# First loads over two queues, a copy moved behind the first products, and another order of the last group's products

## The chip, the cores and the metric

The kernel runs on one core of a Trainium2 chip. The core has a matrix engine (TensorE, PE in the tables), a vector engine (VectorE, DVE), a scalar engine (ScalarE, ACT), a general one (GpSimd, POOL) and SyncE (SP), which only issues transfers. Each engine works through its own list of instructions in order, and the engines wait for one another by semaphores. ACT, SP and POOL can issue DMA transfers: an issue stands in the engine's list like any other instruction. On chip lie SBUF (128 partitions) and PSUM, the small memory into which PE writes and accumulates.

The metric is device time in microseconds (us), the median over several executions; less is better.

## The reference

Two graph layers over N = 4096 nodes with 512 features and one 0/1 adjacency matrix, each followed by a residual and a layer norm. Cut to what matters here, the first layer is:

```
support = (x @ weight).reshape(N, 4, 128)          # 4 heads
f1 = <support, weight_u> per head;  f2 = <support, weight_v> per head
w = leaky_relu(f1[j] + f2[i], 0.2) * adj[i, j]
attn = softmax over j of w, where w != 0
out = attn @ support + bias + x @ proj_w + proj_b
x1 = layernorm(x + out)
```

The second layer is masked attention with 8 heads of 64 over x1, with keys, queries and values from Wks, Wqs, Wvs and an output projection Wo. The change touches the first layer alone, at its very beginning and at the end of its first stage.

## The kernel before

The order of the work on every engine is the order of the program's text (a manual schedule); only semaphores are put in by the framework.

The first stage, the group stage, computes support and the base rows (x + x @ proj_w + biases) for 8 groups of 512 rows (`NG` groups of `GT` = 4 tiles). The two products x @ weight (kind "s") and x @ proj_w (kind "b", where `add_identity`, L888, adds the identity to proj_w so that x itself is included) are each done with a scheme of seven block products instead of eight. So a group has 14 products, named s1 to s7 and b1 to b7, each 8 matmul records on PE (L844). They need sums and differences of weight blocks (`combine_w`, L761, on DVE for "s" and on POOL for "b") and of blocks of x (`combine_x`, L795 to L802). x comes as blocks into `y_sb` (`load_x`, L652) and is turned by 32 x 32 transposes on DVE into `xT` (`turn_x`, L738).

`product` (L844 to L878) runs one product and what follows it. Products 1, 5, 6 and 7 open a PSUM tile (of six, `o_ps`); 2 goes on in the tile of 1, 3 in that of 5, 4 in that of 7. Before 2, 3 or 4 may accumulate, the tile's earlier value must have been read: 1 and 5 are copied out by ACT (L861), 7 is read by a DVE add (L867), and 6 by another (L865). Product 2 is copied by ACT into its place (L863), 3 and 4 are finished by a DVE add (L872). For "b", 3 and 4 end with POOL adding the bias (L876) and SP storing the base rows (L878).

`dots` (L815) is a set of eight dot products on DVE of one quarter of the group's support with u and v, which gives f1 and f2. u and v are spread over all partitions, loaded into `uv` in SBUF and copied once by ACT into PSUM (`uv_ps`, tile x_ps, L901), from where DVE reads them.

The order of the 14 products of a group is a list, `begin` for the first group and `usual` for the others. `todo` puts each quarter's dots a fixed number of places behind the product that completes it. At places 0, 3, 7 and 10 of each list work of later stages is slipped in (`beside`). In the last group place 7 holds two conversions of adjacency (L601, ACT) and `front` of the first three attention steps: ACT computes signs `z` (L628), DVE masks `az` (L632) and the weights `p` (L637).

`factors` follows a group: ACT takes exponentials of f, POOL scales the support (L694 to L698), SP stores it (L701), and DVE turns the factor rows (L708), which SP stores (L713). For all groups but the last it is put off into the next group; for the last it stands right behind the 14 products.

Then come the attention passes: for each step PE multiplies `p` with the scaled support (L1062). In the first pass SP still issues adjacency transposes (L595) for the last pieces of the first window, in its order behind the stores of the last group's `factors`, and ACT converts them (L601) ahead of the steps that use them.

The very first instructions are transfers. SP sends x of group 0 in eight pieces (two halves of four), then the right halves of weight and proj_w in 16 pieces, u, v, and x of group 1. ACT sends the left halves in 16 pieces and the bias. `load_w0` (L661) sends one piece: 64 rows of one half of the columns, 64 KB, into 32 partitions. Then, in the text, DVE turns x of group 0, POOL and DVE combine weights, ACT copies u and v (L901), and the products begin.

Of the kernel before, what the change touches and what calls it, by code (L numbers as in the profile page):

```python
# [12 lines left out]
AF = mybir.ActivationFunctionType  # L13
# [416 lines left out]
def tile_gat_then_masked_attention(  # L430
# [16 lines left out]
    nc = tc.nc  # L447
    N, D = x.shape
    H0, D0, _ = weight_u.shape
# [3 lines left out]
    NG = N // G  # L453
# [15 lines left out]
    SQ = 32  # L469
    NQ = P // SQ  # L470
    HG = G // 2
    HD = D // 2
# [32 lines left out]
    def on_all_partitions(src, n):  # L505
        return bass.AP(tensor=src.tensor, offset=src.offset, ap=[[0, P], [1, n]])
# [63 lines left out]
    with tc.tile_pool(name="l0", bufs=NG) as l0, \  # L570
# [71 lines left out]
        with tc.tile_pool(name="l0s", bufs=2) as sp:  # L642
            w_sb, pw_sb = (sp.tile([P, KC, D], F32, name=n, bufs=1) for n in ("w_sb", "pw_sb"))
            uv = sp.tile([P, 2, D], F32, name="uv", bufs=1)
            ys, xTs = {}, {}

            def load_x(g, b0=0, b1=G // SQ):

                if g not in ys:
                    ys[g] = sp.tile([P, G // SQ, P], F32, name="y_sb", bufs=3)  # L650
                for a in range(NQ):
                    nc.sync.dma_start(  # L652
                        ys[g][a * SQ:(a + 1) * SQ, b0:b1, :],
                        x[g * G + b0 * SQ:g * G + b1 * SQ, a * P:(a + 1) * P].rearrange(
                            "(b r) f -> r b f", r=SQ))

            def load_w0(queue, dst, src, c, m):

                for a in range(NQ):
                    f = a * P + 2 * c * SQ  # L660
                    queue.dma_start(  # L661
                        dst[a * SQ:(a + 1) * SQ, 2 * c:2 * c + 2, m * HD:(m + 1) * HD],
                        src[f:f + 2 * SQ, m * HD:(m + 1) * HD].rearrange("(k r) d -> r k d", r=SQ))

            bb = sp.tile([P, D], F32, name="bb", bufs=1)
            for n in range(2):
                load_x(0, n * HG // SQ, (n + 1) * HG // SQ)
            for queue, m, srcs in ((nc.scalar, 0, ((w_sb, weight), (pw_sb, proj_w))),
                                   (nc.sync, 1, ((w_sb, weight),)),
                                   (nc.sync, 1, ((pw_sb, proj_w),))):  # L670
                for c in range(2):
                    for dst, src in srcs:
                        load_w0(queue, dst, src, c, m)
            nc.scalar.dma_start(bb, on_all_partitions(bias, D))
            nc.sync.dma_start(uv[:, 0, :], on_all_partitions(weight_u, D))
            nc.sync.dma_start(uv[:, 1, :], on_all_partitions(weight_v, D))
            load_x(1)

            def factors(g, s4):
# [83 lines left out]
            def w_of(kind, i):  # L763
                w = w_sb if kind == "s" else pw_sb
                if i in (1, 2, 3):
                    return w_block(w, *{1: (0, 0), 2: (1, 0), 3: (1, 1)}[i])
                return sums_w[kind][{5: 0, 6: 1, 7: 2, 4: 3}[i]]
# [36 lines left out]
            def x_of(g, i):  # L804
                if i in (1, 2, 4):
                    return x_block(g, *{1: (0, 0), 2: (0, 1), 4: (1, 1)}[i])
                return x_s[g][{5: 0, 6: 1, 7: 2, 3: 3}[i]]
# [25 lines left out]
            def product(g, s4, kind, i):  # L833

                if i in (1, 5, 6, 7):
                    tiles[kind, i] = op.tile([P, G], F32, name="o_ps")
                out = tiles[kind, {2: 1, 3: 5, 4: 7}.get(i, i)]
                more = i in (2, 3, 4)  # L840
                xb, wb = x_of(g, i), w_of(kind, i)
                for t in range(2):
                    for c in range(2):
                        nc.tensor.matmul(out[:, t * HD:(t + 1) * HD], xb[:, c, t * P:(t + 1) * P],  # L844
                                         wb[:, c, :], start=not more and t == 0 and c == 0,
                                         stop=c == 1, skip_group_check=True)
                if i == 1:
                    if kind == "b":
                        for n in range(2):
                            base[n] = sp.tile([P, 2, D], F32, name="base", bufs=2)  # L850
                    elif g == NG - 1:
                        places = room("y_sb").rearrange("p s c r -> p s (c r)")
                        sb.update({("s", 1): places[:, 0], ("s", 5): places[:, 1],
                                   ("b", 1): places[:, 2], ("b", 5): places[:, 3]})
                    else:
                        sb.update({("s", 1): room("z"), ("s", 5): room("z"),
                                   ("b", 1): room("az"), ("b", 5): room("az")})
                u2, p5 = sb[kind, 1], sb[kind, 5]
                last = block_of(kind, s4, 1, 1)
                if i in (1, 5):  # L860
                    nc.scalar.activation(sb[kind, i], out, AF.Copy)  # L861
                elif i == 2:
                    nc.scalar.activation(block_of(kind, s4, 0, 0), as_block(out, kind), AF.Copy)  # L863
                elif i == 6:
                    nc.vector.tensor_tensor(u2, out, u2, op=ALU.add)  # L865
                elif i == 7:
                    nc.vector.tensor_tensor(last, as_block(out, kind), as_block(u2, kind),  # L867
                                            op=ALU.add)
                    nc.gpsimd.tensor_tensor(last, last, as_block(p5, kind), op=ALU.add)
                else:  # L870
                    n, m = (0, 1) if i == 3 else (1, 0)
                    nc.vector.tensor_tensor(block_of(kind, s4, n, m), as_block(out, kind),  # L872
                                            as_block(u2, kind), op=ALU.add)
                if kind == "b" and i in (3, 4):
                    n = (3, 4).index(i)
                    nc.gpsimd.tensor_tensor(base[n], base[n],  # L876
                                            bb[:, None, :].to_broadcast([P, 2, D]), op=ALU.add)
                    nc.sync.dma_start(base_d[g][:, 2 * n:2 * n + 2, :], base[n])  # L878
# [18 lines left out]
            combine_w(nc.gpsimd, "b", (5, 6, 7, 4))  # L897
            nc.gpsimd.dma_start(bb, on_all_partitions(proj_b, D), accum_op=ALU.add)
            uv_ps = [xp.tile([P, H0, D0], F32, name="x_ps") for _ in range(2)]
            for k in range(2):  # L900
                nc.scalar.activation(uv_ps[k], uv[:, k, :].rearrange("p (h d) -> p h d", h=H0),  # L901
                                     AF.Copy)
            usual = [(kind, i) for i in (1, 5, 2, 6, 7, 3, 4) for kind in ("s", "b")]
            begin = [("s", 1), ("b", 1), ("s", 2), ("b", 2), ("s", 5), ("s", 6), ("s", 7),
                     ("b", 5), ("s", 3), ("b", 6), ("s", 4), ("b", 7), ("b", 3), ("b", 4)]
            for g in range(NG):
                fs[g] = l0.tile([P, 2, GT, H0], F32, name="f")
                s4 = sp.tile([P, H0, GT, W0], F32, name="s4")
                plan = usual if g else begin
                todo = {}  # L910
                for i, wait, n, m in ((2, 1, 0, 0), (3, 0, 0, 1), (7, 3, 1, 1), (4, 0, 1, 0)):
                    todo.setdefault(plan.index(("s", i)) + wait, []).append((n, m))
                for k, (kind, i) in enumerate(plan):
                    if k in (0, 3, 7, 10):
                        t = (0, 3, 7, 10).index(k)
                        if t == 1 and g + 2 < NG:
                            load_x(g + 2)
                        for fn in beside.get(g * GT + t, []):
                            fn()
                    product(g, s4, kind, i)  # L920
                    for nm in todo.get(k, ()):
                        dots(g, s4, *nm)
                    first = 0 if g else 10
                    if g + 1 < NG and first <= k < first + KC:
                        turn_x(g + 1, k - first)
                    if g + 1 < NG and (6 <= k < 10 if g else k == 13):
                        for n in (k - 6,) if g else range(4):
                            combine_x(g + 1, n)
                    if k in (2, 6, 9, 13):
                        later.step()  # L930
                xTs.pop(g)
                x_s.pop(g)
                if g + 1 < NG:
                    later.at(1, lambda g=g, s4=s4: factors(g, s4))
                else:
                    factors(g, s4)
# [18 lines left out]
        with wait_by_tile("l0v", 2) as vp:  # L955
# [95 lines left out]
            for n, (w, h, j) in enumerate(steps):  # L1051
# [7 lines left out]
                p = p_t.pop((w, h, j))  # L1059
                s = sup[w * H0 + h, j // GT][:, j % GT, :]  # L1060
# [507 lines left out]
```

## Time and profile before

| what | value |
|---|---|
| median of 3 runs | 3373.38 us (3373.2 to 3379.11) |
| the profiled execution's own time | 3375.75 us |
| its span | 3374.0 us |
| PE busy | 3321.3 us, 98% of the span |
| DVE, POOL, ACT busy | 2362.1, 2227.8, 1987.5 us |
| first product on PE | 7.72 us after the span's start |
| last product of the last group | 221.21 us |
| first attention step on PE | 222.93 us |

The span is the time from the first to the last instruction in the profile; the execution's own time lies 1.75 us above it. PE is the engine that is nearly always busy, and the second layer takes most of the span. Matmul ends are modelled, so a busy PE does not mean that its clock is full: the clock that was granted stands in a column of its own in the tables by stretches of time. A row "PE o_ps <- ACT z" in a table of waits says that a PE instruction on tile o_ps was released by an ACT instruction on tile z. A tile name is that of the program; a place can serve under several names (the tile z holds the copy of s1 in the first groups).

### The profile page before, as it was taken

How to read it: one execution, taken by the hardware profiler on the slowest of the kernel's cores; microseconds unless marked ns; L12 is line 12 of the kernel's file. 1: busy time of each engine (PE TensorE's matmuls, PEld its weight loads, DVE VectorE, ACT ScalarE, POOL GpSimd, SP SyncE). 2: the span in 40 equal slices, each digit the busy share in tenths (PEclk: the TensorE clock that was granted, in tenths of full speed). 3: DMA queues.
4: the chain of work that ended last, by engine and by line, in shares of the span. 5: the costliest groups of instructions: out<-in, count | busy, mean ns of one | idle time of the engine just before them, and what ended most of it. 6: DMA issues, size and time to landing. Idle time of an engine off the chain costs nothing.

```text
span 3374.0 us, 66618 instructions
## 1 busy us (share of the span) xinstructions
PE 3321.3 (98%) x27050; PEld 1946.6 (58%) x27050; DVE 2362.1 (70%) x2892; ACT 1987.5 (59%) x2463; POOL 2227.8 (66%) x1590
## 2 busy tenths in 40 slices
PE   7999999999999999999999999999999999999998
PEld 6889999999999855643333333333333333333332
DVE  5678999898898711156766667676676666667666
ACT  1247877878776421155665656656566656656563
POOL 4550031040030275579999999999999999999996
PEclk9999999999999999999999999999999999999999
DMA  7978869769441443388889888889888889798984
GB/s 149 231 163 185 198 184 216 147 161 215 140 130 64 101 162 112 124 217 197 210 191 220 226 209 194 208 196 241 212 189 212 191 207 252 186 210 189 211 195 109
DMA packets 400334, 620.41 MB, mean 184 GB/s; under 512 B 166928, under 2 KB 249872, under 8 KB 398992
## 3 DMA queue, kind: packets, MB, share of 16 engines
q0 software_dynamic: 97520, 258.77, 42.1%
q1 hardware_dynamic: 300544, 354.92, 34.0%
q8 instruction: 215, 3.52, 0.4%
q10 hardware_dynamic: 1952, 2.36, 0.3%
q14 instruction: 103, 0.84, 0.1%
HBM read 315.87 MB, written 117.64 MB: 128 GB/s over the span
## 4 chain that ended last, share of the span: by engine, by line
PE 92%; DMA 3%; POOL 2%; DVE 2%; issue 1%; ACT 1%; SPq 0%; ACTq 0%; POOLq 0%; DVEq 0%
PE o_ps L1062 26%; PE o_ps L1375 24%; PE s_ps L1113 24%; PE s_ps L1178 5%; PE o_ps L844 5%; PE s_ps L1439 3%; PE s_ps L1171 3%; DMA p<-p 2%; POOL q_sum L1350 1%; PE s_ps L1394 1%; DVE p L637 0%; PE x_ps L1043 0%; POOL p L1360 0%; DMA stage<-adj_d 0%; DMA k_d<-v_sb 0%
## 5 line engine op out<-in xcount | busy, mean ns | idle before, releaser
L1350 POOL TENSOR_TENSOR q_sum<-q_sum,p 128x1024 f32<-128x1024 f32 x538 | 1374.5, 2555 | 67.4 <-DMA p<-p 37.2
L1330 DVE TENSOR_TENSOR p<-s_ps,adjT 128x1024 f32<-128x1024 f32 x896 | 1044.6, 1216 | 468.2 <-ACT s_ps L1327 433.2
L1327 ACT ACTIVATE s_ps<-s_ps 128x1024 f32<-128x1024 f32 x1021 | 967.4, 1006 | 599.1 <-PE s_ps L1113 598.9
L1113 PE MATMUL s_ps<-q_sb,k_sb 64*64 64x512 f32 x8192 | 943.3, 589 | 4.2 <-DVE p L1330 4.2
L1375 PE MATMUL o_ps<-p,v_sb 64*64 64x512 f32 x8192 | 943.6, 590 | 0.0
L1062 PE MATMUL o_ps<-sup_t,p 128*128 128x129 f32 x8192 | 920.5, 275 | 6.2 <-DVE p L637 6.1
L1062 PEld LDWEIGHTS o_ps<-sup_t,p 128*128 128x128 f32 x8192 | 917.3, 192 | 7.3 <-DVE p L637 7.2
L637 DVE SCALAR_TENSOR_TENSOR p<-fr_t,dj,az 128x1024 f32<-128x1024 f32 x512 | 656.0, 1291 | 78.6 <-PE o_ps L1062 51.4
L1113 PEld LDWEIGHTS s_ps<-q_sb,k_sb 64*64 64x64 f32 x8192 | 312.2, 133 | 571.2 <-issue 451.2
L1375 PEld LDWEIGHTS o_ps<-p,v_sb 64*64 64x64 f32 x8192 | 310.1, 133 | 570.7 <-issue 560.8
L628 ACT ACTIVATE z<-fr_t,f 128x1024 fp8e4<-128x1024 f32 x512 | 558.0, 1144 | 117.5 <-DVE az L632 117.2
L1360 POOL DMA_DIRECT2D p<-p x412 | 439.0, 1305 | 10.2 <-PE o_ps L1375 8.6
L1026 POOL DMA_DIRECT2D agg<-base_d x32 | 28.7, 1208 | 516.0 <-ACT agg L1012 515.8
L1330 DVE TENSOR_TENSOR p<-s_ps,md 128x1024 f32<-128x1024 f32 x128 | 151.0, 1218 | 68.8 <-ACT s_ps L1327 62.3
L632 DVE TENSOR_TENSOR az<-adjT,z 128x512 int32<-128x512 int32 x256 | 175.7, 686 | 7.5 <-ACT z L628 6.8
L588 POOL COPY seen<-token 128x1 f32<-128x1 f32 x24 | 14.0, 582 | 245.9 <-DVE token L586 245.9
L1185 ACT ACTIVATE sb<-s_ps 128x1024 f32<-128x1024 f32 x35 | 35.8, 1024 | 192.6 <-PE s_ps L1178 129.8
L601 ACT ACTIVATE adjT<-stage 128x1024 fp8e4<-128x1024 bf16 x128 | 130.5, 1050 | 9.2 <-DMA stage<-adj_d 9.2
L1200 POOL TENSOR_TENSOR sb<-sb,sb 128x1024 f32<-128x1024 f32 x36 | 85.0, 2374 | 72.2 <-ACT sb L1185 72.2
L1224 DVE COPY k_sb<-s_ps 128x1024 f32<-128x1024 f32 x12 | 14.7, 1225 | 141.4 <-PE s_ps L1178 91.8
L1439 PE MATMUL s_ps<-wo_sb,on 128*128 128x512 f32 x240 | 110.8, 604 | 0.0
L1409 ACT ACTIVATE r<-r_h 32x256 f32<-32x256 f32 x248 | 102.3, 412 | 2.9
(176 smaller groups left out, 2133.4 us busy)
## 6 DMA issues: line engine op xcount, KB each, us to landing
p<-p POOLq DMA_DIRECT2D x412, 512.0 KB, 9.1
k_sb<-k_d SPq DMA_DIRECT2D x128, 512.0 KB
v_sb<-v_d SPq DMA_DIRECT2D x128, 512.0 KB
adj_d<-in_adj_dram POOLq DMA_DIRECT2D x32, 1024.0 KB, 10.7
sup_t<-sup_d SPq DMA_DIRECT2D x120, 258.0 KB
fr_t<-fr_d SPq DMA_DIRECT2D x16, 1024.0 KB
adjT_d<-adjT SPq DMA_DIRECT2D x32, 512.0 KB
adjT<-adjT_d SPq DMA_DIRECT2D x32, 512.0 KB
```

The lines of the kernel that those rows point to most:

```text
L628: nc.scalar.activation(z[:, k, :], fr[:, 0, :], AF.Sign, bias=fs[j // GT][:, 0, (j + k) % GT, h:h + 1], saturate=False)
L632: nc.vector.tensor_tensor(az.bitcast(I32), adjT[w, j // CJ][:, j % CJ:j % CJ + 2, :].bitcast(I32), z.bitcast(I32), op=ALU.bitwise_and)
L637: nc.vector.scalar_tensor_tensor(p, fr[:, 1, :], dj[j // GT][:, j % GT, h:h + 1], az_t[w, h, j // 2][:, j % 2, :], op0=ALU.max, op1=ALU.mult)
L844: nc.tensor.matmul(out[:, t * HD:(t + 1) * HD], xb[:, c, t * P:(t + 1) * P], wb[:, c, :], start=not more and t == 0 and c == 0, stop=c == ...
L1062: nc.tensor.matmul(o[t // BK][:, t % BK, :], p[:, t * P:(t + 1) * P], s, start=(j == 0 and t % BK == 0), stop=(j == NT - 1), skip_group_ch ...
L1113: nc.tensor.matmul(s[c:c + MS, e, :], k[r, a + c:a + c + MS], qt[g, m][r, :], start=True, stop=True)
L1327: nc.scalar.activation(s, s, AF.Exp)
L1330: nc.vector.tensor_tensor(p, s, keep[:, None, :].to_broadcast([P, HP, G]), op=ALU.mult)
L1350: nc.gpsimd.tensor_tensor(q, q, p, op=ALU.add)
L1360: later.at(2, lambda: nc.gpsimd.dma_start(a, b, accum_op=ALU.add))
L1375: nc.tensor.matmul(o[c, n, :], v[r, j % CH, c], p[r, e, :], start=(j == 0), stop=(j == NT - 1))
L1439: nc.tensor.matmul(s, on_t[g][:, m, t * P:(t + 1) * P], wo_sb[:, m, :], start=(m == 0), stop=(m == NP1 - 1))
```

## The change

Three things change.

- First loads. `load_w0` sends whole rows, 64 rows of all 512 columns, 128 KB in one piece. All 16 pieces go on ACT's queue: the first half of the rows of weight, then of proj_w, then the second halves. u, v and the bias follow on ACT's queue. On SP's queue x of group 1 now follows x of group 0.
- The copies of u and v into PSUM move from ahead of all products to behind the third product (s2) of the first group, ahead of the first dots.
- The last group gets its own order, `end`.

```
-            def load_w0(queue, dst, src, c, m):
+            def load_w0(dst, src, c):
                 for a in range(NQ):
                     f = a * P + 2 * c * SQ
-                    queue.dma_start(
-                        dst[a * SQ:(a + 1) * SQ, 2 * c:2 * c + 2, m * HD:(m + 1) * HD],
-                        src[f:f + 2 * SQ, m * HD:(m + 1) * HD].rearrange("(k r) d -> r k d", r=SQ))
+                    nc.scalar.dma_start(
+                        dst[a * SQ:(a + 1) * SQ, 2 * c:2 * c + 2, :],
+                        src[f:f + 2 * SQ, :].rearrange("(k r) d -> r k d", r=SQ))
...
-            for queue, m, srcs in ((nc.scalar, 0, ((w_sb, weight), (pw_sb, proj_w))),
-                                   (nc.sync, 1, ((w_sb, weight),)),
-                                   (nc.sync, 1, ((pw_sb, proj_w),))):
-                for c in range(2):
-                    for dst, src in srcs:
-                        load_w0(queue, dst, src, c, m)
+            for c in range(2):
+                for dst, src in ((w_sb, weight), (pw_sb, proj_w)):
+                    load_w0(dst, src, c)
+            for k, src in enumerate((weight_u, weight_v)):
+                nc.scalar.dma_start(uv[:, k, :], on_all_partitions(src, D))
             nc.scalar.dma_start(bb, on_all_partitions(bias, D))
-            nc.sync.dma_start(uv[:, 0, :], on_all_partitions(weight_u, D))
-            nc.sync.dma_start(uv[:, 1, :], on_all_partitions(weight_v, D))
             load_x(1)
...
-            for k in range(2):
-                nc.scalar.activation(uv_ps[k], uv[:, k, :].rearrange("p (h d) -> p h d", h=H0),
-                                     AF.Copy)
...
+            end = [("s", 1), ("b", 1), ("s", 5), ("s", 2), ("s", 6), ("s", 7), ("b", 5),
+                   ("s", 3), ("b", 2), ("s", 4), ("b", 6), ("b", 7), ("b", 3), ("b", 4)]
...
-                plan = usual if g else begin
+                plan = end if g == NG - 1 else usual if g else begin
...
                     product(g, s4, kind, i)
+                    if g == 0 and k == 2:
+                        for n in range(2):
+                            nc.scalar.activation(uv_ps[n], uv[:, n, :].rearrange(
+                                "p (h d) -> p h d", h=H0), AF.Copy)
```

## The prediction

> **What bounds the kernel now.** I read first who keeps TensorE (PE) waiting over the whole kernel. A row gives the waiting engine, tile and line, whom it waited for, microseconds in all, times, and the longest.
>
> ```profile
> PE o_ps L844 <- ACT z L861: 14.7, 1, 14.7
> PE o_ps L844 <- DVE xT L738: 7.7, 1, 7.7
> PE o_ps L1062 <- DVE p L637: 6.1, 4, 2.9
> ...
> PE o_ps L844 <- DVE base L867: 1.7, 1, 1.7
> ```
>
> PE is busy 3321.3 of 3374.0 us, so a change that adds no PE work can win only some 50 us. All four rows lie before 263 us; behind that PE hardly waits, so a shift there reaches the end whole. Next, the start: PE's instructions in order of time, then ScalarE's (ACT), each row start, length, engine, line.
>
> ```profile
> 7.72 3.78 PE L844 MATMUL o_ps<-w_sb,xT 128*128 128x256 f32 x8 [7.72 <-DVE xT L738]
> 11.29 1.98 PE L844 MATMUL o_ps<-pw_sb,xT 128*128 128x256 f32 x8
> 28.00 3.78 PE L844 MATMUL o_ps<-w_sb,xT 128*128 128x256 f32 x8 [14.73 <-ACT z L861]
> 31.57 2.08 PE L844 MATMUL o_ps<-pw_sb,xT 128*128 128x256 f32 x8
> ```
> ```profile
> 10.94 0.44 ACTq L674 DMA_DIRECT2D bb<-in_L_gnn_bias_dram  x1
> 11.41 1.28 ACT L901 ACT_TABLE_LOAD   x1 [11.41 <-DMA pw_sb<-in_L_gnn_proj_w_dram]
> 23.93 0.60 ACT L901 ACTIVATE x_ps<-uv 128x512 f32<-128x512 f32 x1 [11.24 <-DMA uv<-in_L_gnn_weight_u_dram]
> 26.83 0.60 ACT L901 ACTIVATE x_ps<-uv 128x512 f32<-128x512 f32 x1 [2.29 <-DMA uv<-in_L_gnn_weight_v_dram]
> 27.36 0.58 ACT L861 ACTIVATE z<-o_ps 128x512 f32<-128x512 f32 x1
> ```
>
> Product s1 was ready at 11.5, but its copy (27.36) stood on ACT behind the two copies of uv, the last data to land. Product s2 accumulates in the same PSUM tile and waited for that copy. PE's restart costs more: s2 took 3.78 us, where later products take 1.89. Stretches of 2 us (last three columns: granted PE clock, DMA share, GB/s) give the clock and the DMA rate.
>
> ```profile
> 8.00:10.00 2.00, 2.00 (x5) 1.56 (x6) 0.64 (x2) 0.00 (x0) 0.00 (x0) 1.00 1.17 201
> 10.00:12.00 2.00, 2.00 (x7) 1.67 (x6) 0.00 (x0) 0.59 (x1) 0.43 (x2) 1.00 1.10 208
> 18.00:20.00 2.00, 0.00 (x0) 0.00 (x0) 2.00 (x3) 0.00 (x0) 1.81 (x2) 0.57 0.52 135
> 28.00:30.00 2.00, 2.00 (x5) 1.64 (x6) 0.00 (x0) 0.43 (x1) 1.05 (x2) 0.50 1.19 194
> ```
>
> DMA runs at 201 to 208 GB/s while x and weights come together, 135 when SP alone sends 64 KB pieces. The mean clock of 0.57 in 18 to 20 puts its fall near 18.3, 5 us after PE's last work at 13.3. Third, the last group, from the timelines of DVE, GpSimd (POOL), SP and PE.
>
> ```profile
> 227.96 3.35 DVE L637 SCALAR_TENSOR_TENSOR p<-fr_t,dj,az 128x1024 f32<-128x1024 f32 x1
> ```
> ```profile
> 227.87 2.35 POOL L876 TENSOR_TENSOR base<-base,bb 128x1024 f32<-128x1024 f32 x1 [2.30 <-DVE base L872]
> ```
> ```profile
> 241.63 12.46 SPq L595 DMA_TRANSPOSE stage<-adj_d  x2
> ```
> ```profile
> 258.76 41.42 PE L1062 MATMUL o_ps<-sup_t,p 128*128 128x129 f32 x365 [1.09 <-DVE p L637]
> ```
>
> DVE ends the group at 227.96 with p of attention step 3. POOL adds the bias to the base rows, scales the support until 238.4, SP stores it, and only then issues the adjacency transposes. Their landing lets ACT go on at 252.5, and PE's last wait here ends at 258.76.
>
> **The change, part by part: first loads.** SP loses 16 weight DMAs and u, v; ACT keeps 16 weight DMAs, of 128 instead of 64 KB, and gains u and v: 16 + 2 + bias = 19 issues, all ahead of its first arithmetic. At 0.44 us each they would take 8.4 us, but issues wait for landings: SP's queue waited 2.3 us for w_sb before x pieces (L652). The first eight issues of both queues together go without such waits, and the ninth on wait, which I read as a count of eight open DMAs shared by both queues. The order along that count seems to follow bytes: by 10.5 us ACT had issued 16 pieces of 64 KB, SP 8 of 128 KB.
>
> Under equal bytes the new order is: 8 pieces of x(0) with 8 of weights; 8 weight pieces with the 4 pieces (256 KB) of x(1); then u, v, bias with x(2). The bias is issue 32 and goes when number 24 has landed. Before that lie 1.05 MB of x(0), three quarters of x(1) (0.79) and 13 weight pieces (1.70), together 3.54 MB; at 205 GB/s that is 17.3 us, from a first flow at 2.2: 19.5. Then 0.4 issue, 1.28 table load, 0.6 copy of s1: s2 starts near 21.7 instead of 28.0, **6.3 us earlier**. s1 and b1 wait for a half and the whole of the first 16 pieces, 0.5 to 1 us later than before; that hides in front of s2. PE is then idle from 14 to 21.7, longer than 5 us, so it restarts cold as before, with no gain there.
>
> Bounds for that start: if whole rows flow at the 404 GB/s of the support loads at 261 to 263, and x at the 194 of 28 to 30, the 3.54 MB take 4.2 + 9.5 = 13.7 and s2 starts at 18.2; a gap of about 4 us may keep the clock, which adds 1.9: gain 11.7. If all of x(1) and x(2) were ahead, 5.2 MB: s2 at 30, loss 2. I take 205, the row with the same mix of loads.
>
> The Trainium skill (DMA: Bandwidth & Descriptors, "Issuing engines are not separate DMA queues") says DMAs of all issuing engines interleave on the same 16 DMA engines. That speaks against a gain from the other queue; by it alone only SP's thin stretch, 16 pieces at 0.45, would be recovered. The Trainium skill (TensorE: Matmul & The Clock Gate, "Why this matters for your kernels") wants no PE gap over about 3 us; by it even the 4 us gap restarts cold, and the fast bound is 9.8.
>
> What else stands behind: add_identity's second half and combine_w on POOL need pw's second half, landing near 23. Then 1.2 + 1.3 + 1.6 + 3.1 + 1.3 (rows of before) give b5's weights at 31.5; b5 is due after s2, b2, s5, s6, s7, at 21.7 + 3.8 + 4 x 1.73 = 32.4. Covered by about 1 us; were pw later than that, it would show one for one.
>
> **Copies of uv after s2.** The two 0.6 us copies move behind s2's copy; u and v land near 25 and 28, s2's copy is at 25.6. b2's copy and the first dots wait behind them until 29; DVE's next due work, s6, comes at 31. Hidden, by 0.5 to 2 us; without that cover DVE slips one for one.
>
> **The last group.** Same instructions, another order: s1 b1 s5 s2 s6 s7 b5 s3 b2 s4 b6 b7 b3 b4. The attention's first weights (front) stay at place 7. (a) Ahead of them ACT now waits for b5, product seven, where it waited for b2, product six: front starts 1.73 later. (b) From there DVE needed 15.0 us to p of step 3 (212.99 to 227.96). One add (s7, 0.61) is now done earlier, but b4 accumulates in b7's tile, and b7's add now stands behind front and all dots. b4 starts when that add ends, takes 1.95, and only b3's add (0.61) fills it: +1.3. So p of step 3 starts 1.73 - 0.61 + 1.3 = 2.4 later. (c) b7's add would end near 227.5. POOL then has 1.1 (L869), 2.3 (b3's bias), and starts b4's bias at 230.9 instead of 227.87: +3.0. Its 10.5 us to the last scaled support, SP's stores and the transposes follow, so 258.76 becomes 261.8: **3.0 us later**. PE's own steps, with DVE 2.4 later, end before that. PE idles some 7 us ahead of b4 and may restart cold; 1.9 at most, covered by that same wait unless DVE's delay shrinks.
>
> Bounds: the dots have four adds fewer ahead (b6, s7, b7, b3: 2.4) and start 1.73 later, so they end 0.7 earlier, and a gain is at most 0.7; cold restart uncovered on top of 3.0 gives a loss of 4.9. I take 3.0, since each piece is a row of this very stage.
>
> **Sum.** 6.3 - 3.0 = 3.3 us. The profiled execution took 3375.75 around its span of 3374.0, 2.4 above the median; by it 3372.4, against the median 3373.38: **3370.1**. A measurement of this kernel tells about 0.2%, 6.7 us, from no change.
>
> **Rivals.**
> *The start wins far more* (28%): weights go ahead of x(1), or whole rows flow fast. With 16 weight and 8 x(0) pieces first, the bias waits for number 20: 2.5 MB, s2 at 16.8, clock kept, gain 12.5 after a short wait for pw; less 3.0: 3363.9. For it: SP and ACT took turns 1 to 2 in number before. Against: that fits equal bytes as well.
> *The last group costs nothing* (12%): POOL finds gaps and the dots' 0.7 counts: 6.3 + 0.7, 3366.4. Against: b7's add behind the dots.
> *Slower* (10%): x(2), issued by SP with nothing in front, gets ahead of the bias, so ACT is held until 28 and s2 starts at 30: -2.0 - 3.0, 3378.4. It decides once the bias is issued after 23 (s2 after 25, gain below 3). Against: 1.25 MB too much would have to come first.
> *Nothing arrives* (5%): later stages take the shift back: 3373. Against: PE has no wait between 52.6 and 199.
> The forecast holds 45%.
>
> **How the numbers follow.** Faster by over 0.2%: the first rival and half of the second, 0.34. Slower by over 0.2% needs the slow rival with the uncovered restart: 0.06. Within: 0.60. Eight in ten reach from the first rival (3363, a little below) to the slow one's near side, 3377; the forecast's own range is 3367 to 3373.
>
> **What would show it.** Right: ACT's table load near 20, s2 near 21.7 at half clock; copies of uv between s2's and b2's copies. In the last group, relative to its s1: PE waits 6 to 7 us for DVE before b4, the transposes are issued 3 later, and PE's last wait ends that much later. Wrong: s2 before 19 at full clock, a table load after 23, or no wait at b4.

## The result, and the profile after

The changed kernel takes 3373.02 us (median of 12 executions, 3370.19 to 3375.19). The kernel before, run beside it, takes 3374.31 us (12 executions, 3371.37 to 3388.86). The ratio is 0.9991, with a 95% interval of 0.9982 to 1.0: no difference that the measurement can tell from none. A later set of runs of the same pair gave 0.9991 again (0.9981 to 1.0001). The forecast of 3370.1 us was 2.9 us too low. The measured time lies inside the eight-in-ten range (3363 to 3377) and just at the upper edge of the forecast's own (3367 to 3373).

Behind "no difference" stand two changes that are both real and cancel. First the waits of TensorE (PE) in the changed kernel, the answer to the table of waits of before (whom it waited for, microseconds in all, times, longest). Lines of this part of the code have moved up by three: the products are L841, their adds on DVE L862, L864 and L869, their copies on ACT L858 and L860.

```profile
PE o_ps L841 <- DVE base L864: 9.2, 2, 7.5
PE o_ps L841 <- DVE xT L735: 8.8, 1, 8.8
PE o_ps L841 <- ACT z L858: 7.5, 1, 7.5
PE o_ps L1062 <- DVE p L637: 2.2, 2, 1.6
```

The wait for the copy of s1 went from 14.7 to 7.5 us. The wait for DVE's add of b7 went from 1.7 us once (in the first group) to 9.2 us in two: a new one of 7.5 us stands in the last group. The waits for `p` went from 6.1 to 2.2: PE now stands still earlier, in front of b4. Next the start, PE and then ACT in order of time (start, length, engine, line).

```profile
8.76 3.78 PE L841 MATMUL o_ps<-w_sb,xT 128*128 128x256 f32 x8 [8.76 <-DVE xT L735]
12.79 2.79 PE L841 MATMUL o_ps<-pw_sb,xT 128*128 128x256 f32 x8 [0.26 <-DMA pw_sb<-in_L_gnn_proj_w_dram]
23.05 3.78 PE L841 MATMUL o_ps<-w_sb,xT 128*128 128x256 f32 x8 [7.46 <-ACT z L858]
26.62 2.64 PE L841 MATMUL o_ps<-pw_sb,xT 128*128 128x256 f32 x8
```
```profile
13.37 4.48 ACTq L661 DMA_DIRECT2D pw_sb<-in_L_gnn_proj_w_dram  x4
18.76 0.36 ACTq L672 DMA_DIRECT2D uv<-in_L_gnn_weight_u_dram  x1
20.74 0.34 ACTq L673 DMA_DIRECT2D bb<-in_L_gnn_bias_dram  x1
21.10 1.28 ACT L858 ACT_TABLE_LOAD   x1 [21.10 <-DMA pw_sb<-in_L_gnn_proj_w_dram]
22.40 0.60 ACT L858 ACTIVATE z<-o_ps 128x512 f32<-128x512 f32 x1
27.36 1.11 ACT L919 ACTIVATE x_ps<-uv 128x512 f32<-128x512 f32 x2
```

ACT issues its 19 DMAs until 20.74 + 0.34 = 21.08, then loads its table and copies s1; the third product, s2, starts at 23.05 instead of 28.00, still at half clock (3.78 us). The copies of u and v now lie at 27.36, back to back, with nothing to wait for. Stretches of 2 us (last three columns: granted PE clock, DMA share, GB/s):

```profile
2.00:4.00 2.00, 0.00 (x0) 0.00 (x0) 0.00 (x0) 0.00 (x0) 0.00 (x0) 1.00 1.01 238
4.00:6.00 2.00, 0.00 (x0) 0.00 (x0) 0.00 (x0) 0.00 (x0) 0.00 (x0) 1.00 1.17 205
10.00:12.00 2.00, 2.00 (x6) 1.45 (x5) 0.00 (x0) 0.00 (x0) 0.73 (x3) 1.00 1.13 197
14.00:16.00 2.00, 1.59 (x6) 1.01 (x5) 1.97 (x5) 0.00 (x0) 0.00 (x0) 1.00 1.15 182
18.00:20.00 2.00, 0.00 (x0) 0.00 (x0) 1.14 (x2) 0.00 (x0) 0.00 (x0) 0.50 1.16 200
28.00:30.00 2.00, 2.00 (x11) 1.77 (x10) 1.78 (x16) 1.07 (x2) 1.92 (x3) 0.97 1.19 188
```

After 238 and 205 GB/s in the first two stretches the transfers run at 182 to 202 GB/s from 6 to 22 us; SP's thin stretch of before (135 GB/s in 18 to 20) is gone. The last group, from the timelines of PE, DVE, POOL, SP and PE again:

```profile
46.48 1.97 PE L841 MATMUL o_ps<-more_w,xT 128*128 128x256 f32 x8 [1.68 <-DVE base L864]
223.42 3.78 PE L841 MATMUL o_ps<-more_w,xT 128*128 128x256 f32 x8 [7.49 <-DVE base L864]
```
```profile
222.67 0.69 DVE L864 TENSOR_TENSOR base<-o_ps,y_sb 128x512 f32<-128x512 f32 x1
223.28 0.68 DVE L869 TENSOR_TENSOR base<-o_ps,y_sb 128x512 f32<-128x512 f32 x1
227.24 0.69 DVE L869 TENSOR_TENSOR base<-o_ps,y_sb 128x512 f32<-128x512 f32 x1 [3.28 <-PE o_ps L841]
228.16 3.35 DVE L637 SCALAR_TENSOR_TENSOR p<-fr_t,dj,az 128x1024 f32<-128x1024 f32 x1
```
```profile
224.82 2.36 POOL L873 TENSOR_TENSOR base<-base,bb 128x1024 f32<-128x1024 f32 x1
228.07 2.35 POOL L873 TENSOR_TENSOR base<-base,bb 128x1024 f32<-128x1024 f32 x1 [0.90 <-DVE base L869]
```
```profile
241.84 12.84 SPq L595 DMA_TRANSPOSE stage<-adj_d  x2
```
```profile
259.48 10.71 PE L1062 MATMUL o_ps<-sup_t,p 128*128 128x129 f32 x90 [1.61 <-DVE p L637]
```

Two fixed points make this readable. The product b4 of the first group (46.48; before 50.87) ends the start; from there to the last group the tables of waits list none of PE in either kernel. PE's last wait of this stage (ending at 259.48; before 258.76) ends the last group. So **the start won 50.87 - 46.48 = 4.4 us, and the last group gave back (259.48 - 46.48) - (258.76 - 50.87) = 213.0 - 207.9 = 5.1 us**: b4 of the last group waited 7.49 us for b7's add (222.67), which stands behind the dots, and then ran at half clock. These are differences of single profiles; e2 below shows that the start of the kernel before scatters by more than 1 us.

The stage thus ends 0.7 us later than before, though the profiled span is 4.9 us shorter (3369.1 against 3374.0). The rest is downstream. The first layer's end costs PE 0.8 us less waiting (PE <- ACT agg at L1178: 1.1 before, 0.3 after), so that both kernels leave the first layer together (L1178 starts at 1157.20, before 1157.25). This goes with the last group's order: the wait is 0.32 us in all six profiles here that have the new order, and 1.09 to 1.10 in the seven with the usual one, so the new order gives 0.8 of its loss back at this place. The second layer, which the change does not touch, had 4.2 us of waits for `p` on its score products in the profile of before and 0.4 here:

```profile
PE s_ps L1113 <- DVE p L1330: 0.4, 1, 0.4
```

Over the profiles of all the kernels below these waits lie anywhere between nothing listed (e6, e10) and 5.1 us (e11). Over 12 executions each, the medians differ by 1.3 us, not by 4.9.

### The profile page after: what moved, and what is told of

Read it like the earlier page. It is cut to its first block, busy times and chain, and to the rows that moved or that the text cites. A ratio compares the mean times of both kernels' runs of the same rounds, so it can differ in the third digit from the quotient of the medians.

```text
span 3369.1 us, 66595 instructions
## 1 busy us (share of the span) xinstructions
PE 3324.9 (99%) x27050; PEld 1950.0 (58%) x27050; DVE 2358.5 (70%) x2892; ACT 1987.4 (59%) x2463; POOL 2226.1 (66%) x1590
## 3 DMA queue, kind: packets, MB, share of 16 engines
q8 instruction: 215, 3.52, 0.4%
## 4 chain that ended last, share of the span: by engine, by line
PE 89%; DMA 1%; DVE 1%; POOL 1%; issue 0%; ACT 0%; POOLq 0%; DVEq 0%; ACTq 0%
PE o_ps L1062 26%; PE o_ps L1375 25%; PE s_ps L1113 25%; PE s_ps L1178 5%; PE s_ps L1439 3%; PE s_ps L1171 3%; DMA p<-p 1%; PE s_ps L1394 1%; PE x_ps L1043 0%; POOL q_sum L1350 0%; DVE p L637 0%; DMA stage<-adj_d 0%; DVE p L1507 0%; PE x_ps L1171 0%; POOL p L1360 0%
## 5 line engine op out<-in xcount | busy, mean ns | idle before, releaser
L1360 POOL DMA_DIRECT2D p<-p x412 | 438.5, 1304 | 10.2 <-PE o_ps L1375 8.5
L1224 DVE COPY k_sb<-s_ps 128x1024 f32<-128x1024 f32 x12 | 14.7, 1225 | 140.7 <-PE s_ps L1178 90.6
## 6 DMA issues: line engine op xcount, KB each, us to landing
adj_d<-in_adj_dram POOLq DMA_DIRECT2D x32, 1024.0 KB, 11.3
```

The lines of the kernel that those rows point to most:

```text
L1360: later.at(2, lambda: nc.gpsimd.dma_start(a, b, accum_op=ALU.add))
```

## The experiments

My theory: the start follows ACT's queue (the copy of s1 comes when ACT has issued its last DMA and, before the change, copied u and v), the last group follows b7's add behind the dots. The rivals: the start follows the bytes or the clock, or differences later in the kernel carry the result. Below, "b4" is the start of b4 in the first group, "end" the end of PE's last wait in this stage, and their difference the cost of all that lies between, which holds the last group's order. Times are medians; ratios are against runs of the kernel before on the same chip.

| kernel | time | ratio (95%) | s2 | b4 | end | end - b4 |
|---|---|---|---|---|---|---|
| before | 3374.31 | 1 | 28.00 | 50.87 | 258.76 | 207.9 |
| changed | 3373.02 | 0.9991 (0.9982 to 1.0) | 23.05 | 46.48 | 259.48 | 213.0 |
| e1 loads and copies | 3368.75 | 0.9978 (0.9969 to 0.9988) | 22.98 | 46.20 | 254.37 | 208.2 |
| e2 last group only | 3377.42 | 1.0006 (0.9997 to 1.0016) | 27.05 | 49.62 | 262.90 | 213.3 |
| e3 copies only | 3362.06 | 0.9959 (0.9944 to 0.9973) | 13.32 | 38.52 | 247.37 | 208.9 |
| e4 loads only | 3374.05 | 0.9999 (0.9989 to 1.0008) | 27.46 | 51.02 | 259.19 | 208.2 |
| e5 kept warm | 3371.16 | 0.9987 (0.9977 to 0.9996) | 23.00 | 45.70 | 258.01 | 212.3 |
| e6 u, v, bias on SP | 3370.56 | 0.9985 (0.9976 to 0.9995) | 19.75 | 45.34 | 258.40 | 213.1 |
| e7 rows on both queues | 3360.28 | 0.9953 (0.9936 to 0.9969) | 16.50 | 37.98 | 246.36 | 208.4 |
| e8 add ahead of dots | 3371.45 | 0.9987 (0.9977 to 0.9996) | 22.95 | 46.62 | 258.04 | 211.4 |
| e9 copies after s5 | 3363.43 | 0.9958 (0.9945 to 0.9972) | 13.47 | 38.62 | 249.31 | 210.7 |
| e10 changed, again | 3372.21 | 0.9991 (0.9981 to 1.0001) | 23.02 | 46.43 | 259.70 | 213.3 |
| e11 copies only, again | 3362.31 | 0.9955 (0.9938 to 0.9971) | 13.40 | 38.72 | 246.64 | 207.9 |

e1 to e4 shared one set of runs of before (median 3374.13), e5 to e8, on another chip, a second (3375.95), and e9 to e11, on the chip of e1 to e4, a third (3374.34). The columns s2, b4 and end come from one profile of each kernel.

### The parts one by one

e1 is the changed kernel without the new order of the last group:

```
-                plan = end if g == NG - 1 else usual if g else begin
+                plan = usual if g else begin
```

> The change without its third part: first loads and late copies of uv as in the changed kernel, the last group in the usual order. Theory (the start gains, the last group gives it back): s2 starts at 23.0 as in the changed kernel, the last group begins 4.4 earlier than before, and PE's last wait of the first pass ends 4.4 earlier than before, near 254.4; total 4.4 below before. Rival (the last group's order is neutral, and the shift is taken back by the adjacency transposes): PE's last wait ends near 258.8 here too, total as before.

Measured: 3368.75 us, 5.4 less than before; s2 and b4 as in the changed kernel, and end - b4 back at 208.2.

e2 is the kernel before with that order alone (the opposite of the two lines above).

> The kernel before with the last group's new order alone. Theory: PE waits some 7.5 us in front of b4, restarts at half clock, and its last wait of the first pass ends 5.1 later than before, near 263.9; total 5.1 above before. Rival (order neutral, the loss in the changed kernel came from elsewhere): last wait near 258.8, total as before.

Measured: 3377.42 us, 3.3 more than before, with an interval that just reaches no change. Its end - b4 is 213.3, 5.4 above before. PE's wait in front of b4 is there without any change at the start:

```profile
226.64 3.78 PE L844 MATMUL o_ps<-more_w,xT 128*128 128x256 f32 x8 [7.57 <-DVE base L867]
262.90 7.37 PE L1064 MATMUL o_ps<-sup_t,p 128*128 128x129 f32 x60 [1.82 <-DVE p L637]
```

e2 has the start of before unchanged, and yet reaches b4 at 49.62, 1.25 us sooner than the profile of before (s2 at 27.05 against 28.00). Against e2 the start of the changed kernel won 3.1 us, not 4.4: so far does this number scatter.

e1 and e2 together show that the two halves act apart: every kernel with the usual order has 207.9 to 208.9 between b4 and end (e9 aside, below), every kernel with the new order and nothing done about it 213.0 to 213.3.

e3 is the kernel before with the copies of u and v behind s2 and no other change:

```
-            for k in range(2):
-                nc.scalar.activation(uv_ps[k], uv[:, k, :].rearrange("p (h d) -> p h d", h=H0),
-                                     AF.Copy)
...
                     product(g, s4, kind, i)
+                    if g == 0 and k == 2:
+                        for n in range(2):
+                            nc.scalar.activation(uv_ps[n], uv[:, n, :].rearrange(
+                                "p (h d) -> p h d", h=H0), AF.Copy)
```

> The kernel before with the copies of uv moved behind s2 alone; loads and last group as before. Theory (what held s2 was the copies' place, and the new loads hold ACT longer than the old ones): ACT is free after its last issue at 11.4, table load to 12.7, s1 copied by 13.3, s2 starts near 13.4 at full clock; s3 waits for the copy of s5 behind the copies of uv (27.4) and starts near 28.5 instead of 40.4; total 11.9 below before. Rival (the whole rows on one queue brought the gain): s2 gains less than 5, because the weights' second halves on SP are late, total at most 4 below before.

e4 is the reverse: the new loads, with the copies ahead of the products as before and the usual order.

> The kernel before with the new first loads alone; copies of uv ahead of all products, last group as before. Theory: u and v land last of all but the bias, so s2 starts at 27.5 to 28.5, total as before within 1. Rival (the whole rows brought the gain): s2 near 23 and total 4.4 below before.

Measured: e3 takes 3362.06 us, 12 less than before, and e4 3374.05, as before. ACT's rows of e3, then of e4:

```profile
10.90 0.44 ACTq L674 DMA_DIRECT2D bb<-in_L_gnn_bias_dram  x1
11.37 1.28 ACT L861 ACT_TABLE_LOAD   x1 [11.37 <-DMA pw_sb<-in_L_gnn_proj_w_dram]
12.66 0.60 ACT L861 ACTIVATE z<-o_ps 128x512 f32<-128x512 f32 x1
```
```profile
20.78 0.45 ACTq L673 DMA_DIRECT2D bb<-in_L_gnn_bias_dram  x1
26.29 0.60 ACT L898 ACTIVATE x_ps<-uv 128x512 f32<-128x512 f32 x1 [0.19 <-DMA uv<-in_L_gnn_weight_v_dram]
26.83 0.58 ACT L858 ACTIVATE z<-o_ps 128x512 f32<-128x512 f32 x1
```

With the loads of before ACT is done issuing at 11.34, so that the moved copies let s1's copy go at 12.66 and s2 at 13.32, at full clock, after a wait of 0.31 us. With the new loads the copies of u and v still have to wait for v, until 26.29: the loads by themselves win nothing. What follows is the main reading of this case: **the move of the copies makes the gain at the start, the new loads bring nothing by themselves and take some 7 us of that gain away** (e3 against e1: 6.7 us of time, 7.7 us at b4), because ACT issues until 21 instead of 11.3 and because the half of weight that s2 needs comes late (e6 and e7 below take the two apart).

One of e3's five executions, the profiled one, took 3373.3. In it PE waits 5.8 us near 366 us, in the attention of the first layer, while in 340 to 360 the transfers moved 92 GB/s against 192 before. I repeated the kernel for that.

> The loads of the kernel before with the copies of u and v behind s2, once more. If its one long execution (3373.3) was an accident of the transfers near 350 us, all executions now lie within 3 us of 3361; if this kernel has two ways of running, one in five lies near 3372 again, with a PE wait of some 6 us near 366.

Measured in e11: four executions between 3359.84 and 3365.47 (the last outside the 3 us expected), no such wait. The long one did not come again; why it came stays open.

### What holds the start

e6 is the changed kernel with u, v and the bias on SP's queue, behind x of group 1:

```
-            for k, src in enumerate((weight_u, weight_v)):
-                nc.scalar.dma_start(uv[:, k, :], on_all_partitions(src, D))
-            nc.scalar.dma_start(bb, on_all_partitions(bias, D))
             load_x(1)
+            for k, src in enumerate((weight_u, weight_v)):
+                nc.sync.dma_start(uv[:, k, :], on_all_partitions(src, D))
+            nc.sync.dma_start(bb, on_all_partitions(bias, D))
```

> The changed kernel with u, v and the bias on SP's queue behind x of group 1, so that ACT has 16 issues instead of 19. Theory (ACT, held by its issues until their turn in the count of landings, sets s2): ACT's last issue ends near 17.9, the table load near 19.2, s2 starts at 19.7 to 20.3 instead of 23.05, and PE's last wait of the first pass ends some 3 earlier, near 256.5. Rival (the second halves of the weights arrive too late for s2): s2 stays near 23 and the rest as in the changed kernel.

Measured: 3370.56 us. The table load follows the last issue at once and s2 starts at 19.75, 3.3 us earlier than in the changed kernel:

```profile
13.32 4.45 ACTq L661 DMA_DIRECT2D pw_sb<-in_L_gnn_proj_w_dram  x4
17.80 1.28 ACT L858 ACT_TABLE_LOAD   x1 [17.80 <-DMA w_sb<-in_L_gnn_weight_dram]
```
```profile
19.75 3.78 PE L841 MATMUL o_ps<-w_sb,xT 128*128 128x256 f32 x8 [4.14 <-ACT z L858]
24.18 3.75 PE L841 MATMUL o_ps<-pw_sb,xT 128*128 128x256 f32 x8 [0.66 <-ACT s L860]
27.73 3.83 PE L841 MATMUL o_ps<-fr_t,p 128*128 128x256 f32 x16
```

So the issue of ACT's last DMA does hold s2. But b4 comes only 1.1 us earlier. The granted clock was 0.5 from 17.9 to 28.2, as in the changed kernel (17.9 to 28.1): s2 and b2 both run at half speed, and s5 starts at 27.73 against 29.10. The time gained ahead of PE's restart was largely spent at half clock. Nor could a still freer ACT have brought s2 much further forward here: s2 also needs the second half of weight, whose last piece landed (the last update of its semaphore in the trace) at 18.70 in e6 and at 18.74 in the changed kernel, having shared the flow with x of group 1.

e7 keeps whole rows of 128 KB but gives the first halves to ACT and the second halves to SP, u and v to SP; the copies are late and the last group's order is the usual one:

```
-            for c in range(2):
+            for queue, c in ((nc.scalar, 0), (nc.sync, 1)):
                 for dst, src in ((w_sb, weight), (pw_sb, proj_w)):
-                    load_w0(dst, src, c)
+                    load_w0(queue, dst, src, c)
             for k, src in enumerate((weight_u, weight_v)):
-                nc.scalar.dma_start(uv[:, k, :], on_all_partitions(src, D))
+                nc.sync.dma_start(uv[:, k, :], on_all_partitions(src, D))
```

> Whole rows, but the first halves of weight and proj_w on ACT and the second halves on SP ahead of u, v and x of group 1; late copies of uv, last group in the usual order. Theory (it is not the whole rows that cost time but the long queue on ACT): ACT is free near 10, s2 starts near 15.2 when weight's second half has landed, s3 near 26.7, as the copies alone gave 27.9; total 12 to 14 below before, PE's last wait of the first pass near 246. Rival (whole rows themselves delay x and so all): s2 after 18, total less than 9 below before.

Measured: 3360.28 us (3357.66 to 3361.78), ratio 0.9953 (0.9936 to 0.9969), the fastest of all, though not to be told from e3 and e11. ACT and PE of e7:

```profile
8.63 0.36 ACTq L673 DMA_DIRECT2D bb<-in_L_gnn_bias_dram  x1
9.02 1.28 ACT L858 ACT_TABLE_LOAD   x1 [9.02 <-DMA pw_sb<-in_L_gnn_proj_w_dram]
12.44 0.60 ACT L858 ACTIVATE z<-o_ps 128x512 f32<-128x512 f32 x1 [2.14 <-PE o_ps L841]
```
```profile
16.50 1.97 PE L841 MATMUL o_ps<-w_sb,xT 128*128 128x256 f32 x8 [1.61 <-DMA w_sb<-in_L_gnn_weight_dram]
37.98 1.97 PE L841 MATMUL o_ps<-more_w,xT 128*128 128x256 f32 x8 [1.69 <-DVE base L864]
```

ACT has issued everything by 9.0 and now waits for PE, not the other way round; s2 waits 1.61 us for the second half of the weights, short enough to keep the clock. The rows are as long as in the changed kernel and the transfers run at 194 to 269 GB/s; two things differ. Ahead of ACT's last issue stands 1 MB of weights here and in e3, 2 MB with u and v in the changed kernel; and the second halves go ahead of x of group 1, so that weight's last piece lands at 16.36, where s2's wait ends. e6 puts the issues of u, v and the bias alone at 3.3 us of s2 (23.05 to 19.75); the other 3.25 us (to 16.50) go with weight's earlier landing. Whole rows by themselves are not what costs: they hold s2 back against e3 (16.50 against 13.32), but b4 is no later for it (37.98 against 38.52).

e9 tries to better e3. There PE waited 1.87 us for the copy of s5, which stood behind the copies of u and v; e9 puts these behind s5 (place 4) and the first dots one place later.

```
-                for i, wait, n, m in ((2, 1, 0, 0), (3, 0, 0, 1), (7, 3, 1, 1), (4, 0, 1, 0)):
+                for i, wait, n, m in ((2, 1 if g else 2, 0, 0), (3, 0, 0, 1), (7, 3, 1, 1), (4, 0, 1, 0)):
...
-                    if g == 0 and k == 2:
+                    if g == 0 and k == 4:
```

> The loads of the kernel before; the copies of u and v stand behind product s5 (place 4) and the first dots one place later, so s5's copy no longer stands behind v. If the 1.87 us wait that PE had in front of s3 at 27.93 with the copies behind s2 comes from the copies alone, s3 starts near 26.1 and the kernel takes 1.9 us less than with the copies behind s2: near 3360, ratio 0.9954 to the kernel before. If DVE is late next instead (its first dots end near 28.7 in both, ahead of the adds of s6 and s7), s4 or b7 waits and at most 0.5 us is won.

Measured: 3363.43 us; one of its six executions took 3798.59 at a granted clock of 0.865, where the others had 0.997 to 0.999, and why stays open. PE of e9:

```profile
26.20 1.89 PE L844 MATMUL o_ps<-w_sb,p 128*128 128x256 f32 x8
30.28 1.99 PE L844 MATMUL o_ps<-fr_t,xT 128*128 128x256 f32 x8 [0.47 <-DVE s L867]
38.62 3.61 PE L844 MATMUL o_ps<-more_w,xT 128*128 128x256 f32 x8 [2.89 <-DVE base L867]
```

The wait is gone and s3 starts at 26.20, as the first expectation says; but DVE is late next, as the second says: b4 starts where it did in e3 (38.62 against 38.52), after a wait of 2.89 instead of 1.68, and at half clock (0.5 from 38.8 to 42.2). It ends 1.7 us later, which is most of the larger end - b4 (210.7). A stall removed in front of a busy engine came back as another, dearer one at this place; the times of e9, e3 and e11 overlap.

### What holds the last group

e5 is the changed kernel with b6's matmuls of the last group run four times over; the last pass overwrites the others, so this is added work that fills part of PE's wait and leaves the order as it is.

```
-                for t in range(2):
+                for t in [t for _ in range(4 if g == NG - 1 and (kind, i) == ("b", 6) else 1)
+                          for t in range(2)]:
```

> The changed kernel, in whose last group the eight matmul records of b6 are made four times over (the same values into the same tile), so that PE works 5.2 longer ahead of its wait for b7's add. Theory (1.9 of the last group's cost is the restart of b4 at half clock): the wait in front of b4 shrinks from 7.5 to 2.3, b4 takes 1.9 instead of 3.8, p of attention step 3 starts 1.8 earlier than in the changed kernel (226.3 instead of 228.2), and PE's last wait of the first pass ends at 257.7 instead of 259.5; total 1.8 below the changed kernel. Rival (the whole cost is DVE's order, the clock is hidden): p of step 3 and the last wait stay within 0.3 of the changed kernel, total the same or higher.

Measured: 3371.16 us. PE, DVE and POOL of e5:

```profile
222.64 1.99 PE L842 MATMUL o_ps<-more_w,xT 128*128 128x256 f32 x8 [2.31 <-DVE base L865]
```
```profile
225.59 1.91 DVE L637 SCALAR_TENSOR_TENSOR p<-fr_t,dj,az 128x1024 f32<-128x1024 f32 x1
```
```profile
224.04 5.67 POOL L874 TENSOR_TENSOR base<-base,bb 128x1024 f32<-128x1024 f32 x2
```

The same line of POOL over the whole kernel (shortest, median and longest in ns, first and last start):

```profile
L874 POOL TENSOR_TENSOR base<-base,bb x16: 2351/2366/3351, 46.9 to 226.4; 128x1024 f32<-128x1024 f32 x16
```

b4 runs at full clock. Counted from the first group's b4, `p` of step 3 starts 1.8 us earlier than in the changed kernel (225.59 - 45.70 = 179.9 against 228.16 - 46.48 = 181.7), but the end only 0.7 (212.3 against 213.0): POOL's two bias additions now run without a pause, but the second, which starts at 226.35 while DVE's `p` is running, takes 3.35 us where it took 2.35. So of the 5.1 us the restart at half clock explains 1.8 on DVE but only 0.7 to 1.0 at the end (212.3 against 213.0 and, in e10, 213.3). With the clock kept, the order still costs 212.3 - 207.9 = 4.4 us.

e8 is the changed kernel with two of the four sets of dots put behind b7, so that b7's add comes ahead of them:

```
-                for i, wait, n, m in ((2, 1, 0, 0), (3, 0, 0, 1), (7, 3, 1, 1), (4, 0, 1, 0)):
+                for i, wait, n, m in ((2, 1, 0, 0), (3, 0, 0, 1), (7, 6 if g == NG - 1 else 3, 1, 1),
+                                      (4, 2 if g == NG - 1 else 0, 1, 0)):
```

> The changed kernel with the last group's last two sets of dots put behind product b7, so that b7's add stands ahead of them on DVE. Theory (b4 waited for b7's add behind the dots): the wait in front of b4 falls from 7.5 to 3.6 or less, b4 starts near 219.5, p of attention step 3 near 224.7 instead of 228.2, PE's last wait of the first pass ends near 257.5; total 2 below the changed kernel. Rival (front at place 7, behind the copy of b5, sets the end, whatever the order of the adds): last wait within 0.5 of 259.5.

Measured: 3371.45 us. PE and DVE of e8:

```profile
220.09 3.45 PE L841 MATMUL o_ps<-more_w,xT 128*128 128x256 f32 x8 [4.01 <-DVE base L864]
```
```profile
224.79 2.76 DVE L637 SCALAR_TENSOR_TENSOR p<-fr_t,dj,az 128x1024 f32<-128x1024 f32 x1
```

The wait in front of b4 falls from 7.49 to 4.01 us, which the two sets of eight dots (1.7 us each, 216.04 to 217.71 in the changed kernel) account for; so it is the dots that b7's add waits behind. `p` of step 3 is 3.5 us earlier (224.79 - 46.62 = 178.2), the end 1.6 (211.4). In place of b7's add, the add of b3 now stands behind the moved dots (it starts at 223.28), and POOL's bias additions begin only at 224.10; I read them as what decides now, without a run that shows it. Against the kernels before, the intervals of e5 and e8 overlap that of the changed kernel: that they are faster than it is shown by the traces only, not by the times.

e10 is the changed kernel unaltered.

> The changed kernel itself beside the others on this chip. If the time follows the issue of ACT's last DMA and the wait at b4, s2 starts within 0.3 us of 23.05, b4 waits 7.4 to 7.6 us, and the ratio to the kernel before is 0.9985 to 0.9998. If the waits of the second layer carried its 4.9 us of span, the ratio scatters to above 1.

Measured: 3372.21 us, 0.9991; s2 at 23.02, the wait 7.49, end - b4 213.3. In these two profiles of the changed kernel the start and the last group repeat to 0.3 us.

## Why the prediction was right, and where it was wrong

**The start.** Right in kind: ACT is held by its issues, the table load comes when the last one is out (21.10, forecast near 20), s2 runs at half clock. Wrong in size: s2 came 4.95 us earlier, not 6.3, and b4 only 4.4 (3.1 against e2). The term that failed is the bias's issue, 20.74 instead of 19.5. The bytes and the rate in it were right: from 2 us on the stretches of the changed kernel add up to 3.52 MB by 19.5, 203 GB/s over 17.3 us, where I had 3.54 MB at 205. So was the count of eight open DMAs: in the trace every issue from the ninth to the bias starts 0.01 to 0.02 us after the landing of the one eight places ahead, though no run varies the count. What the sum left out is the time between a transfer's last packet and its landing, the last update of its semaphore, for which the next issue waits. The last packet of number 24 ended at about 19.7 and it landed at 20.72; for the first 13 pieces of weights, of which it is the last, this step took 0.9 to 1.3 us. I let the issue go with the last byte and put that 1.0 us at nothing; the other 0.2 is the last byte, at 19.7 instead of 19.5. The last 0.55 us went at b2, which took 2.64 us instead of 2.08: the clock came back only at 28.1.

**Which part wins.** Here the working misled. It put 6.3 us under the heading of the loads and called the moved copies "hidden". Hidden they are (27.36, no wait), but moving them away is what frees ACT: e4 gives the loads alone 0, e3 the copies alone 12. The forecast of the start came out near only because both were priced together, against the kernel before; each part against the other was not asked. Had it been, the rows shown ahead of the prediction would have answered: ACT's last issue was out at 11.38 and only u and v stood between it and the copy of s1.

**The last group.** Right in sign and place: PE waits 7.5 us for b7's add (forecast 6 to 7), and the transposes and the last wait move. Forecast +3.0, measured +5.1 (e2: +5.4). The step that failed is the one that called the cold restart of b4 "covered by that same wait". It was not: b4 took 3.78 us, so that b4's add, and with it POOL's bias addition, came 0.90 us after POOL was free (the row at 228.07), and `p` of step 3 came 4.6 us later, not 2.4; with the clock kept (e5) it comes 2.8 later, near the 2.4 worked out. Of the other 1.2 us of the 2.1 missed, 0.7 lies in POOL's earlier operations, which began after b7's add and took 1.27 and 2.36 where 1.1 and 2.3 were put down, and 0.5 in the transposes, whose landing took 11.4 us from the first issue against 10.9 in the profile of before; the profiles of all the kernels here have 10.9 to 11.9, with either order, so these 0.5 are scatter between executions. The bound of 4.9 for an uncovered restart lies near the 5.1 by luck: it adds 1.9 for the restart, of which e5 shows 0.7 to 1.0 at the end.

**The sum.** 6.3 - 3.0 = 3.3 against 4.4 - 5.1 = -0.7 where the stage ends, and 1.3 us between the medians. Both terms missed by about 2 us on the same side, and the scatter of the kernel is as large. That no change would be seen was forecast for a small gain; at the end of the stage there is none. That the time still fell into the range is in part luck: the first layer's end gave 0.8 us back, which was not forecast, and the range is wider than either miss.

**The rivals.** "The start wins far more" fell for this change, since weights and x shared the flow as forecast; that a start at 13 to 17 with the clock kept is worth 12 us is what e3 and e7 show. "The last group costs nothing" fell (e1, e2). "Slower" by x(2) ahead of the bias fell: the bias was out at 20.74, below its point of 23. "Nothing arrives" fell as a mechanism: the 4.4 us won (3.1 against e2) stand at b4 in both profiles of the changed kernel, and it is the last group that takes them; later waits vary by a few microseconds, but in e1, e3 and e7 the gain at b4 (4.7, 12.4 and 12.9) shows in the time (5.4, 12 and 15.7, the last with an interval of 10 to 22).

## What to carry to other kernels

Count what stands in an in-order engine's list ahead of its first needed work: a DMA issue there is not free when it waits for earlier landings, and all of the weights on ScalarE's queue instead of half, with x of the next group beside them on the other, cost this kernel about 7 us, while the same rows split over two queues ahead of that x cost nothing. Where an issue waits for a landing, price the landing and not the last byte (here some 1 us later). Price each part of a change alone and against the others: here one of three parts, the moved copies, was worth 12 us, and the other two spent it. A wait of TensorE of some 2 us or more may have to be priced with a restart at half clock behind it (1.9 us were enough in three profiles here, 2.9 were not in another), and what hangs on the restarted product has to be followed to the end before the restart is called covered.

## What was not expected of the hardware

The clock of TensorE fell sooner than read from the profile of before. There it fell 5 us after PE's last work; in the changed kernel it fell 2.3 us after (work ended at 15.6, half clock from 17.9), and in the last group 3.4 us after (215.9 to 219.3). Even a gap of 2.9 us cost the clock in e7, e3 and e11 and not in the kernel before, where PE stood still from 228.5 to 231.4 and kept it; and gaps of 1.9 us cost it in e5, e8 and e10 (half clock from 258.7, 233.3 and 260.2, some 0.5 to 0.7 us after PE had gone on), while one of 2.1 us in e3, ahead of 247.37, did not. Ahead of the program's end the stretches at half clock were 3.4, 6.8, 10.2 or 13.7 us long in all these traces, multiples of 3.4. The Trainium skill (TensorE: Matmul & The Clock Gate, "Part 1: The HAM clock gate (the "warmup" mystery)") describes a free-running activity window of about 3.4 us, and these lengths agree with it; the start of such a window relative to the gap would then decide whether a gap of 2 to 5 us costs the clock, which no run here isolates. The column of the granted clock has to be read with care at the very beginning: the traces hold no clock record before 10.9 to 17.4 us, and the column reads 1.00 there, while the first product took 3.4 to 3.8 us in every profile, where later ones take 1.89.

POOL's addition of 128x1024 took 2.36 us alone (224.82 in the changed kernel), and DVE's `p` 1.28 (214.12). Where they met, the one that began second took longer: in the changed kernel POOL began first, at 228.07, and took 2.35, while `p`, from 228.16, took 3.35; in e5 POOL's second addition began at 226.35 while `p` was running and took 3.35. This was in a stage where both engines lie on the path.
